# A two-layer block (attention, then a selective scan) on one core: the order of the layer norm, the score maxima, the first scan chunk and the gates is changed

## Chip, cores and metric

The kernel runs on one core of a Trainium2 chip. The metric is the device time in microseconds (us) of one execution, median over runs. The engines are PE (TensorE), DVE (VectorE), ACT (ScalarE), POOL (GpSimd) and SP (SyncE, which issues most DMAs); each takes its instructions strictly in its program's order.

## What is computed

There are 4 sequences of 256 tokens, model width 512. Layer 0 is an attention with 32 heads of latent key width 4, beside a feed-forward block of width 1792. Layer 1 is a selective scan (inner width 1024, 16 states, convolution of 4 taps), beside a top-2 mixture of low-rank experts on a dense product. The reference, cut:

```python
xn = layernorm(x)
x = x + attn(xn) + ffn(xn)
xn = layernorm(x)
x = x + scan_block(xn) + experts(xn)

# attn: scores = einsum(q, C_kv) / 2; softmax; @ V; @ Wo
# ffn:  (silu(xn @ Wg.T) * (xn @ Wu.T)) @ Wd.T
# scan_block:
xi, z = split(xn @ in_proj)               # 2 x 1024 channels
xc = silu(conv4(xi) + conv_b)
dt_r, Bm, Cm = rmsnorm of the parts of (xc @ x_proj.T)
dt = softplus(dt_r @ dt_proj.T + dt_bias)
h = exp(dt * A) * h + dt * Bm * xc        # along the 256 tokens, 1024 x 16 states
y = (sum over states of h * Cm + D * xc) * silu(z)
out = y @ out_proj.T
```

## The kernel before, in words

Everything is in one program with an order written out by hand. No scheduler moves anything: each engine runs its instructions in the order in which the code issues them. Tiles come from pools with tags; a tile with a tag and `bufs=2` takes the older of two buffers, and its first writer waits until the last readers of that buffer are done. The PSUM pool `psmm` has three buffers for most products, `pssc` two for scores.

*Layer 0.* Tokens stand in eight blocks of 128; two sequences (four blocks) are a half. Products of the feed-forward block are cut into small pieces: `gate_up(th)` and `down(th, i)` are generators, and `go(ff, n)` issues the next n pieces on PE between other work. A piece of `down` is two matmuls (hi and lo part, L454); each block of `down` begins with four matmuls of the attention's output against `m_att` (L449) and ends with an addition into x on DVE (L459).

For the softmax a maximum over the keys is needed. `scores_max` (L337, L339) makes scores of two groups of heads on PE and reduces them on DVE into `mpl`; eight steps k with two reduces each. `put_max(b, gq)` (L349, L356) transposes `mpl` with PE (`pmT`) and adds the masked maxima into `qg` on DVE; it needs two steps' maxima. `maxima(b, pieces, second, side)` runs the eight steps for a first sequence of a half with `pieces[k]` pieces of `ff` in step k; `attention(b, ff, after, step)` runs the eight steps of one sequence's softmax with the maxima of the next sequence in between.

The layer norm of a half: `ln_stats`, `ln_root` (ACT square root), `ln_scale` (DVE reciprocal L213, then one DVE instruction for each block, L216), `ln_turn` (PE transposes L225, ACT copies into `xhi` and `xnT`, L227 and L228) and `ln_rest` (DVE, `xlo`, L234). For the second half this stands after the attention of sequence 1, among the first pieces of `down(0)`, together with `normalize(1)`: four reciprocals of softmax denominators and four products on DVE (L398, L399). Then come `latents(2)` with nine pieces and `maxima(2)`.

*Layer 1.* A sequence b is worked through in 8 chunks c of 128 channels; each chunk has four steps g of four states, so a sequence has 32 scan steps (PER) and the kernel 128. A step u: `decays(u)` (four exponentials on ACT, L930), `scan_in(u)` (`bx` on DVE, L936), `scan(u)` (the scan `h` on DVE, L951, then `hc` = h times C on POOL, L955), `states_sum(u)` (`ysum` on PE, L967). After four steps `close_chunk` multiplies with the gate on DVE (`xc`, L971). A chunk's dt and du = dt*xc must lie with each channel repeated for the four states: `send` writes them to DRAM (`dtd`, `dud`) and `spread` reads them back in four DMAs each (`dts`, `dus`, L889). For the very first chunk the code before the loop instead uses PE with a selection matrix (`pdts` L1143, `pdus` L1150) and copies on DVE (L1146, L1152).

Other work is hung on steps with `put(b, s, f, ...)` and `put_late`: what is put on step s is issued around scan s, in the order of the calls, late ones after the others. For sequence 0 these are, among others: `load_z` and `pz_mm` (weights and product of the gate z, L898) and `gate_silu` (ACT, L904, with a change of the activation table before and after it, the second at L688) for chunk pairs 0 and 1; `norm_stats`, `norm_scale` (L713, tiles `xnt`), `norm_turn` (PE `pt`, L721) and `norm_copy` (L729) for the next sequence; `step_in` (PE `pdt` L820, ACT L825 and L826), `step_exp` (ACT L834 to L837) and `step_out` (POOL) for dt of the second half of the channels; `step_x` (`du` on POOL, L875); `px_mm`, `conv_in` (ACT) and `conv_taps` (DVE L761) for the next sequence. The tiles `xnt` and `du` have the same tag, `xnt`, with two buffers.

The tail of `down(1)`, for the last blocks of layer 0, is spread between the first matmuls of layer 1, and runs until the first scans are under way. SP issues the weight loads `w_in` (three buffers) in its order with the other DMAs; POOL issues those of the gate and up weights `wgu`.

In the last scan step `scan(u, parts)` is called with four parts, so that each quarter's `hc` follows that quarter's scan.

Of the kernel before, what the change touches and what calls it, by code (L numbers as in the profile page):

```python
# [8 lines left out]
F32 = mybir.dt.float32  # L9
# [3 lines left out]
ALU = mybir.AluOpType  # L13
# [4 lines left out]
P = 128  # L18
# [23 lines left out]
def block_kernel(  # L42
# [167 lines left out]

    def ln_scale(th, i, n):
        mv, rs = tok[th][2:]
        nc.vector.reciprocal(rs[:, i : i + n], rs[:, i : i + n])  # L213
        for k in range(i, i + n):
            xn = ap1.tile([P, D], F32, tag="ln_xn", name="xn", bufs=2)
            nc.vector.tensor_scalar(  # L216
                xn, x[:, 4 * th + k, :], mv[:, k, 0:1], rs[:, k : k + 1], ALU.subtract, ALU.mult
            )
            tok[th, k] = xn

    def ln_turn(th, i):
# [257 lines left out]
    def attention(b, ff, after, step, side=()):  # L479


        side = dict(side)
        for k in range(8):
            attend(b, k, 0)
            if after:
                scores_max(b + 1, k, 1 - k // 2 % 2)
            elif k:
                attend(b, k, 1)
            if after or k == 0:
                go(ff, step - step // 2)  # L490
            if k == 0:
                put_max(b, 3)
                go(ff, 3)
            elif after and k % 2 == 0:
                put_max(b + 1, k // 2 - 1)
            if after or k == 0:
                attend(b, k, 1)
            if after:
                scores_max(b + 1, k, k // 2 % 2)
            if k:  # L500
                weigh(b, k - 1)
            elif b % 2:
                weigh(b - 1, 7)
            go(ff, step // 2 if after or k == 0 else step)
            for f, *args in side.get(k, ()):
                f(*args)
# [32 lines left out]
    def maxima(b, pieces, second, side=()):  # L539

        side = dict(side)
        for k in range(8):
            for hp in range(2):
                scores_max(b, k, hp)
            for f, *args in side.get(k, ()):
                f(*args)
            go(ff, pieces[k])
            if k and k % 2 == 0:
                put_max(b, k // 2 - 1)
            go(second, 1)  # L550
        go(second)
# [17 lines left out]
    go(ff)  # L569
    ff = (0 for i in range(4) for _ in down(0, i))  # L570
    go(ff, 4)
    next(norm)
    for i in range(4):
        ln_turn(1, i)
        go(ff, 2)
        next(norm)
        if i == 1:
            ln_scale(1, 2, 2)
        ln_rest(1, i)
        go(ff, 1)  # L580
    first, second = latents(2), latents(3)
    for i in range(9):
        go(first, 1)
        go(ff, 1)
        if i == 5:
            pre_stats(0)
    maxima(2, (4, 4, 4, 6, 4, 4, 4, 4), second, {
        2: [(pre_stats, 1)], 3: [(pre_scale,)], 5: [(pre_turn, 0)], 7: [(pre_turn, 1)],
    })
    go(ff)  # L590
# [17 lines left out]
    w_of = {("x", 0, 0): weights(inx_d, 0)}  # L608
    vec = we.tile([P, DC, V_END], F32, name="vec")
    nc.sync.dma_start(vec, vec_d)  # L610
    w_of["x", 0, 1] = weights(inx_d, 2)
    w_of["x", 0, 2] = weights(inx_d, 4)
    xpw = we.tile([P, DC, 64], F32, name="xpw")
    lnw = we.tile([64, 1], F32, name="lnw")
    dtw = we.tile([RK, DIN], F32, name="dtw")
    norm = normalize(3)
    next(norm)
    go(ff, 4)
    for _ in norm:
        go(ff, 2)  # L620
    go(ff)
    ffs.close()
    ps0.close()
# [317 lines left out]
    def scan(u, parts=1):  # L941
# [7 lines left out]
        for k in range(parts):  # L949
            n = slice(k * NG // parts, (k + 1) * NG // parts)  # L950
            nc.vector.tensor_tensor_scan(  # L951
                h[:, n].rearrange("p n t -> p (n t)"), da[:, n].rearrange("p n t -> p (n t)"),
                bx[:, n].rearrange("p n t -> p (n t)"), 0.0, ALU.mult, ALU.add,
            )
            nc.gpsimd.tensor_tensor(  # L955
                hc[:, n], h[:, n],
                crows[b][:, g, :].unsqueeze(1).to_broadcast([P, NG // parts, S]), ALU.mult,
            )
# [139 lines left out]
    for i in range(2):  # L1098
# [5 lines left out]
    nc.scalar.activation(xcs[0][:, 0:6, :], xcs[0][:, 0:6, :], AF.Silu)  # L1104
    nc.scalar.activation(xcs[0][:, 6:8, :], xcs[0][:, 6:8, :], AF.Silu)
    exp_set()

    sel = w1.tile([P, KC - 1, S], F32, tag="tap", name="sel").rearrange("p k t -> p (k t)")
    nc.vector.tensor_copy(
        sel[:, 0 : NG * P].rearrange("p (k n j) -> p k n j", k=NG, n=NG),  # L1110
        ident.rearrange("p (k j) -> p k j", k=NG).unsqueeze(2).to_broadcast([P, NG, NG, NB]),
    )
    for n in range(NG):
        w = slice(n * NB, (n + 1) * NB)
        nc.scalar.activation(
# [15 lines left out]
    u, e, lw = live["u"], live["e"], live["lw"]  # L1131
    dt = dts[0, 0]
    du = w1.tile([P, 2, S], F32, tag="xnt", name="du", bufs=2)
    for j, eng in ((0, nc.vector), (1, nc.gpsimd)):
        eng.tensor_tensor(e[:, j, :], u[:, j, :], e[:, j, :], ALU.subtract)
        eng.tensor_tensor(e[:, j, :], e[:, j, :], lw[:, j, :], ALU.add)
        eng.tensor_tensor(dt[:, j, :], dt[:, j, :], e[:, j, :], ALU.add)
        eng.tensor_tensor(du[:, j, :], dt[:, j, :], xcs[0][:, j, :], ALU.mult)
    go(ff, 5)

    pdts = psx.tile([P, NG, S], F32, tag="bx", name="pdts")
    for k in range(NG):
        mm(pdts[:, k, :], lhsT=sel[:, k * P : (k + 1) * P], rhs=dt[:, 0, :], start=True, stop=True)  # L1143
    live["dts", 0, 0] = w1.tile([P, NG, S], F32, tag="dts", name="dts", bufs=2)
    live["dus", 0, 0] = w1.tile([P, NG, S], F32, tag="dus", name="dus", bufs=2)
    nc.vector.tensor_copy(live["dts", 0, 0], pdts)  # L1146
    for i in range(2):
        pdu = psmm.tile([P, 2, S], F32, tag="mm", name="pdus")
        for k in range(2):
            mm(pdu[:, k, :], lhsT=sel[:, (2 * i + k) * P : (2 * i + k + 1) * P], rhs=du[:, 0, :],  # L1150
               start=True, stop=True)
        nc.vector.tensor_copy(live["dus", 0, 0][:, 2 * i : 2 * i + 2, :], pdu)  # L1152
    for n, t in (("dt", dt[:, 1, :]), ("du", du[:, 1, :])):
        live[n, 0, 0] = scr.tile([2, P, S], F32, tag=n, name=f"{n}d")
        nc.sync.dma_start(live[n, 0, 0][1], t)
    decays(0)
    scan_in(0)
    spread("dt", 0, 1)
# [31 lines left out]
    for b in range(B):  # L1190
# [14 lines left out]
        else:  # L1205
            put(b, 1, one_out, 2)
            put(b, 1, one_step, 3)
            put(b, 2, one_out, 3)
            put_late(b, 2, load_z, b, 0)
            put_late(b, 2, lambda: send("dt", 0, 1, dts[0, 0][:, 2:4, :]))  # L1210
            put_late(b, 2, step_x, b, 1)
            put(b, 4, load_z, b, 1)
            for k, n in enumerate(("rl", "bw", "lb", "ow")):
                put(b, 9 + 2 * k, load_late, n)
            for p, u in ((0, 3), (1, 8)):
                for i in range(2):
                    put(b, u, pz_mm, b, p, i)
            put(b, 4, gate_silu, b, 0)
            put(b, 12, gate_silu, b, 1)
            put_late(b, 1, add_last, 5)  # L1220
            put_late(b, 3, add_last, 6)
            put_late(b, 4, add_last, 7)
# [23 lines left out]
        if nxt < B:  # L1246
            o = 0 if b else 1
            put(b, 0 if b else 2, norm_stats, nxt)
            put(b, 2 if b else 4, norm_scale, nxt)
            put(b, 3 if b else 5, norm_turn, nxt, 0)  # L1250
            (put if b else put_late)(b, 4 if b else 5, norm_copy, nxt, 0)
            put(b, 4 if b else 5, norm_turn, nxt, 1)
            (put if b else put_late)(b, 5, norm_copy, nxt, 1)
            for p in range(NP):
                put(b, 2 * p if b else (5, 6, 9, 9)[p], load_x, nxt, p)
                for i in range(2):
# [182 lines left out]
```

## Time and profile before

| | |
|---|---|
| time, median of 3 runs | 862.01 us (856.58 to 865.05) |
| time of the profiled execution | 866.83 us |
| its span, first to last instruction | 865.1 us |
| PE busy | 736.6 us (85%) |
| DVE busy | 685.6 us (79%) |
| ACT busy | 526.5 us (61%) |
| POOL busy | 489.6 us (57%) |
| mean granted PE clock | 0.918 |
| scans on DVE, L951 | 288.0 us in 129 instructions |
| wait of PE for hc in front of ysum | 79.2 us in 59 waits |

The time of the profiled execution is 1.7 us over its span. Lines of a timeline give the start, the duration, the engine, the source line and operation, out<-in with the shapes, how many instructions are taken together, and in square brackets the idle time of the engine before them with what ended it. Lines of the table by stage give a stretch of the span, its length, then busy time and number of instructions of PE, PE's weight loads, DVE, ACT and POOL, then the granted PE clock (1.00 is full), the share of the DMA engines and the GB/s.

### The profile page before, as it was taken

To read this page: it belongs to the slowest core of one execution; us is meant where nothing else is said; L and a number is where in the kernel's file an instruction comes from. 1 tells how busy PE (TensorE), PEld (TensorE's weight loads), DVE (VectorE), ACT (ScalarE), POOL (GpSimd) and SP (SyncE) were. 2 spreads that over 40 slices of the span, in tenths; PEclk is the share of its full clock that TensorE was granted. 3 is DMA by queue.
4 is the path that set the end of the run, shared out by engine and by line. 5 is a ranking of instruction groups with operands and counts; after the bars stand their busy time and mean duration, and the time that the engine had idled before them with its cause. 6 is when DMAs were issued, how large, how long until landed. Compare 5 with 4: busy or idle time off the path is not lost.

```text
span 865.1 us, 10769 instructions
## 1 busy us (share of the span) xinstructions
PE 736.6 (85%) x3702; PEld 411.7 (48%) x3702; DVE 685.6 (79%) x684; ACT 526.5 (61%) x1011; POOL 489.6 (57%) x377
## 2 busy tenths in 40 slices
PE   5989998989999999897877997677988778957965
PEld 3665544666555667554433454334345434312422
DVE  4687755477734437778999999999999999999995
ACT  4315574224556377687794877794976784955451
POOL 3223331001333335569759699669699659697664
PEclk9999999989999999987879899779999878988995
DMA  7234322001233323547532556233535233326200
GB/s 219 76 83 123 95 76 61 1 1 37 74 86 86 104 42 86 137 134 227 161 98 85 147 146 147 85 98 111 167 101 156 76 97 106 101 77 181 73 25 24
DMA packets 67200, 86.68 MB, mean 100 GB/s; under 512 B 12061, under 2 KB 52009, under 8 KB 66762
## 3 DMA queue, kind: packets, MB, share of 16 engines
q1 hardware_dynamic: 57786, 67.12, 27.9%
q0 software_dynamic: 9072, 18.35, 7.6%
q8 instruction: 29, 0.48, 0.2%
q10 hardware_dynamic: 288, 0.52, 0.2%
q14 instruction: 25, 0.20, 0.1%
HBM read 66.58 MB, written 10.22 MB: 89 GB/s over the span
## 4 chain that ended last, share of the span: by engine, by line
PE 42%; DVE 34%; ACT 10%; POOL 7%; issue 5%; DMA 1%; DVEq 0%; SPq 0%; ACTq 0%; POOLq 0%
DVE h L951 20%; DVE bx L936 6%; PE pg L429 6%; PE pu L429 6%; ACT decay L930 6%; PE po L454 4%; POOL hc L955 4%; PE av L382 4%; PE px L737 3%; PE pz L898 2%; PE scT L371 2%; PE ysum L967 2%; DVE mpl L339 2%; PE po L1059 2%; PE pp L781 2%
## 5 line engine op out<-in xcount | busy, mean ns | idle before, releaser
L955 POOL TENSOR_TENSOR hc<-h,cr 128x1024 f32<-128x1024 f32 (+1 forms) x131 | 302.2, 2310 | 103.3 <-DVE h L951 85.5
L951 DVE TENSOR_TENSOR_SCAN h<-decay,bx 128x1024 f32<-128x1024 f32 (+1 forms) x129 | 288.0, 2234 | 15.6 <-PE po L454 4.0
L930 ACT ACTIVATE decay<-dts,aneg 128x255 f32<-128x255 f32 x504 | 213.5, 498 | 118.9 <-DVE h L951 108.5
L967 PE MATMUL ysum<-hc,stack 128*32 128x256 f32 x1024 | 93.8, 437 | 79.6 <-POOL hc L955 79.2
L936 DVE TENSOR_TENSOR bx<-brow,dus 128x1024 f32<-128x1024 f32 x128 | 157.6, 1231 | 3.7
L441 POOL TENSOR_TENSOR hlo<-g,hhi 128x512 fp32r<-128x512 f32 x28 | 35.9, 1281 | 119.9 <-ACT hhi L440 119.9
L967 PEld LDWEIGHTS ysum<-hc,stack 128*32 128x32 f32 x1024 | 22.0, 114 | 142.7 <-POOL hc L955 123.4
L339 DVE TENSOR_REDUCE mpl<-sc 128x4 f32<-128x1024 f32 x64 | 76.7, 1219 | 12.5 <-PE sc L337 12.3
L412 POOL DMA_DIRECT2D wgu<-in_wgu x56 | 31.2, 557 | 96.9 <-PE pg L429 94.8
L373 ACT ACTIVATE pe<-scT 128x1024 f32<-128x1024 f32 x64 | 64.0, 1023 | 23.4 <-PE sc L337 15.1
L1059 PE MATMUL po<-ow,xc 128*128 128x512 f32 x128 | 73.0, 680 | 2.2 <-DVE xc L971 2.2
L898 PE MATMUL pz<-xn1T,w_in 128*128 128x256 f32 x256 | 68.0, 413 | 0.0
L737 PE MATMUL px<-xn1T,w_in 128*128 128x256 f32 x256 | 65.8, 406 | 0.8 <-ACT xn1T L729 0.8
L737 PEld LDWEIGHTS px<-xn1T,w_in 128*128 128x128 f32 x256 | 51.6, 204 | 19.3 <-issue 9.1
L898 PEld LDWEIGHTS pz<-xn1T,w_in 128*128 128x128 f32 x256 | 49.1, 201 | 19.2 <-issue 12.2
L437 DVE SCALAR_TENSOR_TENSOR g<-g,pg 128x512 f32<-128x512 f32 x28 | 19.2, 687 | 41.6 <-ACT g L436 41.6
L454 PE MATMUL po<-wd,hhi 128*128 128x512 f32 x112 | 50.6, 452 | 0.0
L429 PE MATMUL pu<-xhi,wgu 128*128 128x512 f32 x112 | 48.2, 431 | 1.8 <-DMA wgu<-in_wgu 1.8
L429 PE MATMUL pg<-xhi,wgu 128*128 128x512 f32 x112 | 48.7, 435 | 0.0
L440 ACT CAST hhi<-g 128x512 fp32r<-128x512 f32 x28 | 17.3, 619 | 48.8 <-DVE g L439 48.8
L454 PE MATMUL po<-wd,hlo 128*128 128x512 f32 x112 | 45.4, 405 | 0.0
L429 PE MATMUL pu<-xlo,wgu 128*128 128x512 f32 x112 | 45.2, 403 | 0.0
(223 smaller groups left out, 1218.5 us busy)
## 6 DMA issues: line engine op xcount, KB each, us to landing
dts<-dtd SPq DMA_DIRECT2D x124, 128.0 KB, 2.8
dus<-dud SPq DMA_DIRECT2D x124, 128.0 KB, 3.0
wgu<-in_wgu POOLq DMA_DIRECT2D x56, 256.0 KB, 2.8
w_in<-in_inx SPq DMA_DIRECT2D x16, 512.0 KB, 4.4
w_in<-in_inz SPq DMA_DIRECT2D x16, 512.0 KB, 5.5
dtd<-dt SPq DMA_DIRECT2D x15, 256.0 KB, 2.2
dud<-du SPq DMA_DIRECT2D x15, 256.0 KB, 2.2
wd<-in_wd POOLq DMA_DIRECT2D x7, 512.0 KB, 3.5
```

Source lines behind the costliest of these rows:

```text
L339: nc.vector.tensor_reduce(mpl2[b % 2][:, qb, 2 * hp : 2 * hp + 2, 16 + 2 * gq : 18 + 2 * gq], sc.rearrange("p i (f k) -> p i f k", f=2), A ...
L373: nc.scalar.activation(pes[b, k][:, 2 * t : 2 * t + 2, :], sc, AF.Exp)
L429: mm(ps, lhsT=wgus[i][:, hc, :], rhs=xs[j][:, hc, :], start=(hc == 0 and j == 0), stop=(hc == HC - 1 and j == 1))
L454: mm(po, lhsT=hids[th][j][:, m, i * P : (i + 1) * P], rhs=wd[:, m, :], start=False, stop=(m == MC - 1 and j == 1))
L737: mm(px[:, i, :], lhsT=w[:, i, hc, :], rhs=xns[b][:, hc, :], start=(hc == 0), stop=(hc == HC - 1))
L898: mm(pz[:, i, :], lhsT=w[:, i, hc, :], rhs=xns[b][:, hc, :], start=(hc == 0), stop=(hc == HC - 1))
L930: nc.scalar.activation(da[:, k, 1:], live["dts", b, c][:, k, 1:], AF.Exp, scale=aneg[:, c, k, g : g + 1])
L936: nc.vector.tensor_tensor(bx, brow[g // 2][:, g % 2, :].unsqueeze(1).to_broadcast([P, NG, S]), live["dus", b, c], ALU.mult)
L951: nc.vector.tensor_tensor_scan(h[:, n].rearrange("p n t -> p (n t)"), da[:, n].rearrange("p n t -> p (n t)"), bx[:, n].rearrange("p n t -> ...
L955: nc.gpsimd.tensor_tensor(hc[:, n], h[:, n], crows[b][:, g, :].unsqueeze(1).to_broadcast([P, NG // parts, S]), ALU.mult,)
L967: mm(ysum[k * NB : (k + 1) * NB, :], lhsT=stack, rhs=hc[:, k, :], start=False, stop=(g == NU - 1))
L1059: mm(live["po", b, i], lhsT=xcs[b][:, c, i * P : (i + 1) * P], rhs=late_w["ow"][:, c, :], start=False, stop=(c == DC - 1))
```

## The change

1. In `attention` and `maxima` the three later `put_max` calls come at k = 3, 5 and 7 instead of 2, 4 and 6.
2. Second half of layer 0's norm: one reciprocal for all four blocks; the blocks 2 and 3 are scaled on ACT (new function `ln_scale_act`) and not on DVE. `normalize(1)` is run to its end before the transposes, with nine pieces of `down(0)` in between; each transposed block is followed by three pieces.
3. `maxima(2)` runs with 26 pieces instead of 34.
4. The calls that load the second and third `w_in` tile come between the steps of `normalize(3)`.
5. The first chunk's dt and du go through DRAM like the others; the selection matrix, its 16 matmuls and the three copies are gone.
6. For sequence 0, `norm_scale` of the next sequence comes late in step 2, ahead of `step_x`, instead of in step 4; `norm_turn` in step 4 for both blocks; the second `load_z` in step 3 instead of 4, its `pz_mm` in step 5 instead of 8, its `gate_silu` in step 7 instead of 12.
7. In `scan` the last part's `hc` is made on DVE when a step is run in four parts.

```diff
@@ -210,12 +210,27 @@
 
     def ln_scale(th, i, n):
         mv, rs = tok[th][2:]
-        nc.vector.reciprocal(rs[:, i : i + n], rs[:, i : i + n])
+        if th == 0 or i == 0:
+            m = n if th == 0 else 4
+            nc.vector.reciprocal(rs[:, i : i + m], rs[:, i : i + m])
         for k in range(i, i + n):
             xn = ap1.tile([P, D], F32, tag="ln_xn", name="xn", bufs=2)
             nc.vector.tensor_scalar(
                 xn, x[:, 4 * th + k, :], mv[:, k, 0:1], rs[:, k : k + 1], ALU.subtract, ALU.mult
             )
+            tok[th, k] = xn
+
+    def ln_scale_act(th, i, n):
+
+        mv, rs = tok[th][2:]
+        sh = ap1.tile([P, 4], F32, tag="ln_sh", name="sh")
+        nc.vector.scalar_tensor_tensor(
+            sh[:, 0:n], mv[:, i : i + n, 0], -1.0, rs[:, i : i + n], ALU.mult, ALU.mult
+        )
+        for k in range(i, i + n):
+            xn = ap1.tile([P, D], F32, tag="ln_xn", name="xn", bufs=2)
+            nc.scalar.activation(xn, x[:, 4 * th + k, :], AF.Identity, bias=sh[:, k - i : k - i + 1],
+                                 scale=rs[:, k : k + 1])
             tok[th, k] = xn
 
     def ln_turn(th, i):
@@ -491,7 +506,7 @@
             if k == 0:
                 put_max(b, 3)
                 go(ff, 3)
-            elif after and k % 2 == 0:
+            elif after and k in (3, 5, 7):
                 put_max(b + 1, k // 2 - 1)
             if after or k == 0:
                 attend(b, k, 1)
@@ -545,7 +560,7 @@
             for f, *args in side.get(k, ()):
                 f(*args)
             go(ff, pieces[k])
-            if k and k % 2 == 0:
+            if k in (3, 5, 7):
                 put_max(b, k // 2 - 1)
             go(second, 1)
         go(second)
@@ -569,22 +584,23 @@
     go(ff)
     ff = (0 for i in range(4) for _ in down(0, i))
     go(ff, 4)
-    next(norm)
+    for n in (1, 2, 2):
+        for _ in range(n):
+            next(norm)
+        go(ff, 3)
     for i in range(4):
         ln_turn(1, i)
-        go(ff, 2)
-        next(norm)
         if i == 1:
-            ln_scale(1, 2, 2)
+            ln_scale_act(1, 2, 2)
+        go(ff, 3)
         ln_rest(1, i)
-        go(ff, 1)
     first, second = latents(2), latents(3)
     for i in range(9):
         go(first, 1)
         go(ff, 1)
         if i == 5:
             pre_stats(0)
-    maxima(2, (4, 4, 4, 6, 4, 4, 4, 4), second, {
+    maxima(2, (4, 3, 3, 5, 3, 3, 3, 2), second, {
         2: [(pre_stats, 1)], 3: [(pre_scale,)], 5: [(pre_turn, 0)], 7: [(pre_turn, 1)],
     })
     go(ff)
@@ -608,16 +624,16 @@
     w_of = {("x", 0, 0): weights(inx_d, 0)}
     vec = we.tile([P, DC, V_END], F32, name="vec")
     nc.sync.dma_start(vec, vec_d)
-    w_of["x", 0, 1] = weights(inx_d, 2)
-    w_of["x", 0, 2] = weights(inx_d, 4)
     xpw = we.tile([P, DC, 64], F32, name="xpw")
     lnw = we.tile([64, 1], F32, name="lnw")
     dtw = we.tile([RK, DIN], F32, name="dtw")
     norm = normalize(3)
     next(norm)
     go(ff, 4)
-    for _ in norm:
+    for i, _ in enumerate(norm):
         go(ff, 2)
+        if i in (1, 3):
+            w_of["x", 0, i // 2 + 1] = weights(inx_d, i + 1)
     go(ff)
     ffs.close()
     ps0.close()
@@ -952,7 +968,8 @@
                 h[:, n].rearrange("p n t -> p (n t)"), da[:, n].rearrange("p n t -> p (n t)"),
                 bx[:, n].rearrange("p n t -> p (n t)"), 0.0, ALU.mult, ALU.add,
             )
-            nc.gpsimd.tensor_tensor(
+
+            (nc.vector if k == NG - 1 else nc.gpsimd).tensor_tensor(
                 hc[:, n], h[:, n],
                 crows[b][:, g, :].unsqueeze(1).to_broadcast([P, NG // parts, S]), ALU.mult,
             )
@@ -1104,12 +1121,6 @@
     nc.scalar.activation(xcs[0][:, 0:6, :], xcs[0][:, 0:6, :], AF.Silu)
     nc.scalar.activation(xcs[0][:, 6:8, :], xcs[0][:, 6:8, :], AF.Silu)
     exp_set()
-
-    sel = w1.tile([P, KC - 1, S], F32, tag="tap", name="sel").rearrange("p k t -> p (k t)")
-    nc.vector.tensor_copy(
-        sel[:, 0 : NG * P].rearrange("p (k n j) -> p k n j", k=NG, n=NG),
-        ident.rearrange("p (k j) -> p k j", k=NG).unsqueeze(2).to_broadcast([P, NG, NG, NB]),
-    )
     for n in range(NG):
         w = slice(n * NB, (n + 1) * NB)
         nc.scalar.activation(
@@ -1131,28 +1142,19 @@
     u, e, lw = live["u"], live["e"], live["lw"]
     dt = dts[0, 0]
     du = w1.tile([P, 2, S], F32, tag="xnt", name="du", bufs=2)
+    for n in ("dt", "du"):
+        live[n, 0, 0] = scr.tile([2, P, S], F32, tag=n, name=f"{n}d")
     for j, eng in ((0, nc.vector), (1, nc.gpsimd)):
         eng.tensor_tensor(e[:, j, :], u[:, j, :], e[:, j, :], ALU.subtract)
         eng.tensor_tensor(e[:, j, :], e[:, j, :], lw[:, j, :], ALU.add)
         eng.tensor_tensor(dt[:, j, :], dt[:, j, :], e[:, j, :], ALU.add)
+        nc.sync.dma_start(live["dt", 0, 0][j], dt[:, j, :])
         eng.tensor_tensor(du[:, j, :], dt[:, j, :], xcs[0][:, j, :], ALU.mult)
+        nc.sync.dma_start(live["du", 0, 0][j], du[:, j, :])
+        if j == 0:
+            spread("dt", 0, 0)
+            spread("du", 0, 0)
     go(ff, 5)
-
-    pdts = psx.tile([P, NG, S], F32, tag="bx", name="pdts")
-    for k in range(NG):
-        mm(pdts[:, k, :], lhsT=sel[:, k * P : (k + 1) * P], rhs=dt[:, 0, :], start=True, stop=True)
-    live["dts", 0, 0] = w1.tile([P, NG, S], F32, tag="dts", name="dts", bufs=2)
-    live["dus", 0, 0] = w1.tile([P, NG, S], F32, tag="dus", name="dus", bufs=2)
-    nc.vector.tensor_copy(live["dts", 0, 0], pdts)
-    for i in range(2):
-        pdu = psmm.tile([P, 2, S], F32, tag="mm", name="pdus")
-        for k in range(2):
-            mm(pdu[:, k, :], lhsT=sel[:, (2 * i + k) * P : (2 * i + k + 1) * P], rhs=du[:, 0, :],
-               start=True, stop=True)
-        nc.vector.tensor_copy(live["dus", 0, 0][:, 2 * i : 2 * i + 2, :], pdu)
-    for n, t in (("dt", dt[:, 1, :]), ("du", du[:, 1, :])):
-        live[n, 0, 0] = scr.tile([2, P, S], F32, tag=n, name=f"{n}d")
-        nc.sync.dma_start(live[n, 0, 0][1], t)
     decays(0)
     scan_in(0)
     spread("dt", 0, 1)
@@ -1207,16 +1209,17 @@
             put(b, 1, one_step, 3)
             put(b, 2, one_out, 3)
             put_late(b, 2, load_z, b, 0)
+            put_late(b, 2, norm_scale, nxt)
             put_late(b, 2, lambda: send("dt", 0, 1, dts[0, 0][:, 2:4, :]))
             put_late(b, 2, step_x, b, 1)
-            put(b, 4, load_z, b, 1)
+            put(b, 3, load_z, b, 1)
             for k, n in enumerate(("rl", "bw", "lb", "ow")):
                 put(b, 9 + 2 * k, load_late, n)
-            for p, u in ((0, 3), (1, 8)):
+            for p, u in ((0, 3), (1, 5)):
                 for i in range(2):
                     put(b, u, pz_mm, b, p, i)
             put(b, 4, gate_silu, b, 0)
-            put(b, 12, gate_silu, b, 1)
+            put(b, 7, gate_silu, b, 1)
             put_late(b, 1, add_last, 5)
             put_late(b, 3, add_last, 6)
             put_late(b, 4, add_last, 7)
@@ -1246,11 +1249,12 @@
         if nxt < B:
             o = 0 if b else 1
             put(b, 0 if b else 2, norm_stats, nxt)
-            put(b, 2 if b else 4, norm_scale, nxt)
-            put(b, 3 if b else 5, norm_turn, nxt, 0)
-            (put if b else put_late)(b, 4 if b else 5, norm_copy, nxt, 0)
-            put(b, 4 if b else 5, norm_turn, nxt, 1)
-            (put if b else put_late)(b, 5, norm_copy, nxt, 1)
+            if b:
+                put(b, 2, norm_scale, nxt)
+            put(b, 3 if b else 4, norm_turn, nxt, 0)
+            (put if b else put_late)(b, 4, norm_copy, nxt, 0)
+            put(b, 4, norm_turn, nxt, 1)
+            (put if b else put_late)(b, 5 if b else 4, norm_copy, nxt, 1)
             for p in range(NP):
                 put(b, 2 * p if b else (5, 6, 9, 9)[p], load_x, nxt, p)
                 for i in range(2):
```

## Prediction

> **What bounds the kernel now.** I read the page first, then the busy time by stage, then the timelines of the engines around each edit.
>
> ```profile
> PE 736.6 (85%) x3702; PEld 411.7 (48%) x3702; DVE 685.6 (79%) x684; ACT 526.5 (61%) x1011; POOL 489.6 (57%) x377
> PE 42%; DVE 34%; ACT 10%; POOL 7%; issue 5%; DMA 1%; DVEq 0%; SPq 0%; ACTq 0%; POOLq 0%
> ```
>
> ```profile
> 131.00:152.00 21.00, 18.26 (x83) 10.43 (x76) 11.53 (x21) 8.85 (x15) 1.97 (x3) 1.00 0.22 60
> 152.00:202.00 50.00, 46.15 (x233) 32.10 (x231) 30.91 (x44) 10.92 (x20) 0.00 (x0) 0.90 0.00 1
> 283.00:356.00 73.00, 70.06 (x298) 51.05 (x297) 40.21 (x56) 41.29 (x86) 30.02 (x44) 1.00 0.32 85
> 356.00:420.00 64.00, 51.75 (x271) 32.59 (x269) 54.48 (x44) 53.45 (x109) 50.89 (x34) 0.83 0.64 185
> 420.00:850.00 430.00, 345.17 (x1704) 168.28 (x1704) 411.85 (x327) 302.74 (x636) 332.12 (x181) 0.89 0.39 106
> ```
>
> The columns are PE, PEld, DVE, ACT, POOL, clock, DMA. Up to 356 PE sets the pace (70.06 of 73 us). From 420 on DVE does (411.85 of 430), so a delay at the start of the scan is not won back. Between lies the entry, 356 to 420, where no engine is full and waits decide. I call 355.46, where PE ends its down loop and starts pz, T0.
>
> ```profile
> 186.07 0.44 PE L349 MATMUL pmT<-cst,mpl 128*128 128x128 f32 x2 [1.80 <-DVE mpl L339]
> 336.43 1.88 PE L449 MATMUL po<-m_att,o8n 128*128 128x512 f32 x4
> 341.34 0.64 PE L967 MATMUL ysum<-hc,stack 128*32 128x256 f32 x8
> 355.46 3.62 PE L898 MATMUL pz<-xn1T,w_in 128*128 128x256 f32 x16
> 374.45 3.72 PE L898 MATMUL pz<-xn1T,w_in 128*128 128x256 f32 x16
> ```
>
> ```profile
> 355.72 2.29 DVE L951 TENSOR_TENSOR_SCAN h<-decay,bx 128x1024 f32<-128x1024 f32 x1 [3.95 <-PE po L454]
> 361.24 2.28 DVE L951 TENSOR_TENSOR_SCAN h<-decay,bx 128x1024 f32<-128x1024 f32 x1
> 380.54 0.42 DVE L971 TENSOR_TENSOR xc<-ysum,sz 128x256 f32<-128x256 f32 x1 [4.72 <-PE ysum L967]
> 385.82 2.29 DVE L951 TENSOR_TENSOR_SCAN h<-decay,bx 128x1024 f32<-128x1024 f32 x1
> ```
>
> Scan 4 cannot start before T0, scan 5 starts at T0+5.8, and scan 10 at T0+30.4. The second pz, at 374.45, stands in front of the ysum for which DVE waits 4.72.
>
> **The change, part by part** (us; minus is a gain).
>
> *Maxima a step later.* A put_max transposes maxima whose second half comes from the reduces of its step. At k=3, 5, 7 those are still the two newest reduces (1.18 each). PE waits for them 5.1 in all (the waits view), and two score buffers make PE wait for reduces anyway. In the first maxima loop the transposes now stand behind 6, 5 and 4 pieces instead of 1, 1 and 5; of one wait of 2.2 I take 0.6 (bounds −2.5 to +0.5).
>
> *Second half of the norm.* Before, PE waited 0.52, 0.94 and 0.51 for xlo and 0.78 for x between 141 and 149, because four reciprocals (0.95) with products (0.29) stood among DVE's norm work. Now they come first, covered by nine pieces. Blocks 2 and 3 go to ACT, 0.81 each by its Identity rows on such tiles, and DVE loses 2×0.5. The latents start at about 153.3 instead of 151.1, with 25 pieces done instead of 16: 9×0.46 = 4.15, less 2.2, is −1.9. The third maxima loop gets 26 pieces for 34 and took 37.7; with those 4.15 gone DVE is its bound (16 reduces 18.7, adds, copies and products 9, and the waits at its ends), some 31.4. Of the 6.3, 4.15 are the pieces counted already and 1.0 returns as m_att in the latents loop: −1.1. Together −3.0 (bounds −6 to −0.5). With maxima, **−3.6** (−8 to 0).
>
> *Weight loads 2 and 4 later.* The order of SP's instructions and their waits are the same in both programs: **0**. If the loads did start later, PE's one wait of 1.8 for wgu at 289.14 might go: −1.8.
>
> *First chunk through DRAM.* PE loses 16 matmuls: 3.5 on PE's path. DVE loses 2.5 of copies and the 0.4 selector. Instead SP issues two more stores and eight more reads. Chunk 1 made that trip already:
>
> ```profile
> 331.24 0.34 SPq L1155 DMA_DIRECT2D dtd<-dt  x1
> 332.05 0.32 SPq L1155 DMA_DIRECT2D dud<-du  x1
> 332.96 1.76 SPq L889 DMA_DIRECT2D dts<-dtd  x4
> 334.81 1.32 SPq L889 DMA_DIRECT2D dus<-dud  x3
> ```
>
> Its dts had landed at 337.09 and its dus at 339.40, 5.85 and 8.16 after the first issue. DVE's dt ends at 327.77, so dts is there at 333.7 and dus at 336.0. decays(0) on ACT then ends at 335.5, and behind it in ACT's queue stands the copy cr, which frees the psmm buffer that PE's m_att needs: PE runs dry at 332.9 and goes on at 336.15, against 336.43. So the 3.5 turn into a wait. h0 moves from 334.55 to 337.4, its hc (2.29+2.37) ends at 342.1, and PE waits there for ysum until 342.1 instead of 341.34. The end of the loop comes at T0 **+1.0** (from −3.5, if ACT's queue frees cr in time, to +2.7, if the clock falls).
>
> Here the clock matters. After the wait of 1.80 at 186.07 the granted clock fell, while after the 1.80 at 289.14 it stayed at 1.00:
>
> ```profile
> 186.60:193.40 6.80, 6.73 (x28) 5.66 (x28) 3.35 (x6) 0.59 (x1) 0.00 (x0) 0.50 0.00 0
> 287.50:291.00 3.50, 1.86 (x8) 1.42 (x8) 3.47 (x4) 1.11 (x2) 1.27 (x1) 1.00 0.07 20
> ```
>
> One stretch of 3.4 at half clock costs 1.7 where PE is the bound; that is the +2.7, and the sum would be 868.2 instead of 866.5. Of two waits of one length one did it; I take no fall and keep the bound. The Trainium skill, "TensorE: Matmul & The Clock Gate", section "What's actually happening", lets the clock fall only after an idle window of about 3.4 us, by which 3.25 of idle would leave the sum at 866.5; but the wait of 1.80 at 186.07 is far short of that window and the clock fell, so the trace does not bear the rule out.
>
> *The gates and the norm of the next half at the entry.* xnt and du share two buffers. norm_scale now comes ahead of step_x, so POOL's du (1.28) waits for PE's transposes pt, which stand behind pz (3.55) and a ysum (0.55). Counted from the loop's new end: pt done 4.7, du 6.1. Behind du on POOL stand the memsets of two decay tiles, hc3 and hc4 (2.37 each); on SP the store of du, the second load of pz weights, and chunk 2's reads. hc3 ends at 8.7, its ysum at 9.2, xc at 9.6, so scan 5 starts at 9.6 instead of 5.8: +3.8. That is not the worst. The weight load issues at 6.6. This load took 4.08 and 6.63 in the two rows of the entry; the second, at 352.43, ran beside reads like these, and I take it: 13.2. PE reaches that pz in its fifth step, idle from 9.2, ends it at 16.7, and only then makes the pdt that ACT needs. ACT's ledger follows. Before, it ran without a pause from 355.66 to the taps of conv_in, which end at 382.88 (T0+27.4). Now xnt leaves (−1.5), the second silu with two table loads comes in (1.28+0.60+1.28 = +3.2), and ACT stands still from 9.5 to 17.3 (+7.8): 36.9. DVE had covered 1.5 of ACT's lateness at 383.07, so scan 10 moves by +9.5−1.5 = **+8.0**. The bounds: +5, with the short landing; +11.5, with a half-clock pz (+3.5). The gain, the second pz out of DVE's way at 380.54 (4.72), is inside this, since DVE now waits for ACT there.
>
> Later, step 12 is free of that silu: its stall of 0.35 at 400.86 goes, **−0.35** (−2.1 if the 1.73 at 411.30 went too; 0 at worst).
>
> *Last quarter on VectorE.* POOL's last quarter ends at 856.06, DVE's scan at 854.64; a quarter takes POOL 0.69, and DVE 0.42 by its products of that size (L971), so three quarters on POOL end last, at 855.4. **−0.5** (−0.7 to 0).
>
> The sum is −3.6 +1.0 +8.0 −0.35 −0.5 = +4.5. The profiled run (866.83, its span 865.1) would become 871.3; it lies above the median of 862.01, so against the median it is **866.5**.
>
> **Rivals.**
> 1. *The clock and the load go wrong together* (slower). PE's idle from 9.2 to 13.2 drops the clock for pz, and the loop has lost a stretch too: +11.5 and +2.7, with −0.5 upstream and −0.85 at the ends: 874.9. It decides once PE is idle some 4 us in front of the second pz. For it: the clock is 0.83 over 356 to 420 already. Against: the wait at 289.14 left no mark.
> 2. *The du buffer does not hold POOL* (faster). If du goes through before the transposes, the load issues as early as before, the 4.72 at 380.54 vanishes, and the entry gives −4.7: −3.6+1.0−4.7−0.85, 853.9. Against: two buffers, three tiles in that order.
> 3. *PE's saving arrives* (faster). cr is copied in time, the loop ends 3.5 earlier, upstream gives its full 8, and the entry costs its least, 5: 854.7. Against: ACT's order, decays before cr.
> 4. *The moved loads act after all*, −1.8: 864.7. Against: SP's order is unchanged.
>
> **How the numbers follow.** Chances: forecast 0.60, first rival 0.25, second 0.05, third 0.07, fourth 0.03. Three timings of the kernel before span 8.5 us, so 1% (8.6) is what a measurement can tell from no change. The forecast's own range is 861 to 871, nearly all within 1%. Slower by over 1%: 0.22 of the first rival and 0.06 of the forecast's upper end, 0.28. Faster by over 1%: some two thirds of the second and third rival, 0.09 with the forecast's lower end. The rest, 0.63, is within. The range, 857 to 877, takes in the first rival and leaves out most of the two fast ones.
>
> **What would show it.** Right: PE idle about 3 us in front of m_att of the second block of down(1); h0 near 337 less the upstream gain; DVE at scan 5 waiting for ysum or memset; ACT idle some 8 us ahead of L841; DVE waiting some 9 us for ACT's xc ahead of scan 10. Wrong: POOL's du before PE's pz; the second pz starting without a DMA wait; the distance from the first pz to scan 10 under 34 us. The latents starting no later than 151 with as many pieces, or the third maxima loop still at 37 us, would upset the upstream gain.

## Result, and the profile after

The changed kernel takes 872.25 us (median of 4 runs, 871.29 to 874.74) against 863.53 (856.58 to 868.9): a ratio of 1.0114, 95% interval 1.0069 to 1.0158. Timed again later (the run `after_again` below) it took 872.41 against 860.75, 1.0146 (1.0113 to 1.0178). It is slower by 1.1 to 1.5%.

The head of the page hides this: every engine is busy for no longer than before, or nearly so. In the chain, DVE's share fell from 34 to 31% and DMA's rose from 1 to 4%.

```profile
PE 730.9 (84%) x3686; PEld 407.1 (47%) x3686; DVE 682.0 (78%) x679; ACT 527.9 (61%) x1013; POOL 488.8 (56%) x376
PE 42%; DVE 31%; ACT 11%; POOL 6%; issue 6%; DMA 4%; SPq 0%; DVEq 0%; ACTq 0%; POOLq 0%
```

The table by stage (columns as before) shows the place. From 356 to 420 DVE is busy for 46.10 us instead of 54.48, PE for 42.17 instead of 51.75: both wait.

```profile
131.00:152.00 21.00, 20.52 (x92) 13.59 (x91) 9.94 (x18) 8.92 (x15) 1.81 (x2) 1.00 0.14 39
152.00:202.00 50.00, 45.85 (x251) 31.05 (x249) 35.27 (x51) 13.84 (x23) 0.53 (x1) 0.97 0.02 6
283.00:356.00 73.00, 68.01 (x274) 48.50 (x275) 35.83 (x47) 44.00 (x93) 27.29 (x38) 0.95 0.27 64
356.00:420.00 64.00, 42.17 (x229) 27.06 (x228) 46.10 (x39) 45.83 (x94) 46.60 (x33) 0.87 0.68 176
420.00:850.00 430.00, 343.72 (x1715) 168.07 (x1713) 412.06 (x327) 305.62 (x640) 333.64 (x185) 0.90 0.41 111
```

The timelines show who waits for whom, one fence for each engine: PE, POOL, SP, ACT, DVE.

```profile
332.26 3.67 PE L464 MATMUL po<-m_att,o8n 128*128 128x512 f32 x4 [2.85 <-ACT cr L826]
353.10 3.62 PE L914 MATMUL pz<-xn1T,w_in 128*128 128x256 f32 x16
361.73 0.64 PE L984 MATMUL ysum<-hc,stack 128*32 128x256 f32 x8 [3.42 <-POOL hc L972]
365.83 5.73 PE L914 MATMUL pz<-xn1T,w_in 128*128 128x256 f32 x16 [3.46 <-DMA w_in<-in_inz]
```

```profile
358.04 1.26 POOL L891 TENSOR_TENSOR du<-dt,xc 128x512 f32<-128x512 f32 x1 [9.94 <-PE pt L737]
359.33 4.66 POOL L972 TENSOR_TENSOR hc<-h,cr 128x1024 f32<-128x1024 f32 x2
```

```profile
359.33 0.37 SPq L899 DMA_DIRECT2D dud<-du  x1
359.87 0.35 SPq L621 DMA_DIRECT2D w_in<-in_inz  x1
```

```profile
372.71 0.47 ACT L841 ACTIVATE u<-pdt,vec 128x256 f32<-128x256 f32 x1 [10.23 <-PE pdt L836]
```

```profile
353.35 2.29 DVE L967 TENSOR_TENSOR_SCAN h<-decay,bx 128x1024 f32<-128x1024 f32 x1 [2.37 <-PE po L469]
362.85 2.28 DVE L967 TENSOR_TENSOR_SCAN h<-decay,bx 128x1024 f32<-128x1024 f32 x1
391.39 1.01 DVE L777 SCALAR_TENSOR_TENSOR px<-pad,vec,px 128x256 f32<-128x256 f32 x2 [8.28 <-ACT xc L764]
394.17 2.29 DVE L967 TENSOR_TENSOR_SCAN h<-decay,bx 128x1024 f32<-128x1024 f32 x1
```

Read in the order of causes: POOL's du waits 9.94 for the transposes pt; with it wait the hc behind it (PE 3.42 in front of ysum) and the weight load behind du's store (PE 3.46 in front of the second pz). The granted clock is 0.50 from 363.5 to 370.0, and that pz takes 5.73 instead of 3.7. ACT has had nothing to do for 10.23 when the pdt behind it comes, and DVE waits 8.28 for ACT in front of scan 10. From the first pz to scan 10 it takes 41.07 us; before, 30.36.

### The profile page after: what moved, and what is told of

Its sections match the earlier page's. It is cut to its first block, busy times and chain, and to the rows that moved or that the text cites. A ratio compares the mean times of both kernels' runs of the same rounds, so it can differ in the third digit from the quotient of the medians.

```text
span 870.9 us, 10749 instructions
## 1 busy us (share of the span) xinstructions
PE 730.9 (84%) x3686; PEld 407.1 (47%) x3686; DVE 682.0 (78%) x679; ACT 527.9 (61%) x1013; POOL 488.8 (56%) x376
## 4 chain that ended last, share of the span: by engine, by line
PE 42%; DVE 31%; ACT 11%; POOL 6%; issue 6%; DMA 4%; SPq 0%; DVEq 0%; ACTq 0%; POOLq 0%
DVE h L967 18%; DVE bx L952 6%; PE pg L444 6%; ACT decay L946 6%; PE pu L444 6%; PE po L469 5%; POOL hc L972 4%; PE av L397 4%; PE pz L914 3%; PE scT L386 2%; PE px L753 2%; PE ysum L984 2%; DVE mpl L354 2%; PE po L1076 2%; PE po L464 2%
## 5 line engine op out<-in xcount | busy, mean ns | idle before, releaser
L984 PE MATMUL ysum<-hc,stack 128*32 128x256 f32 x1024 | 91.7, 429 | 92.1 <-POOL hc L972 91.7
```

The lines of the kernel that those rows point to most:

```text
L984: mm(ysum[k * NB : (k + 1) * NB, :], lhsT=stack, rhs=hc[:, k, :], start=False, stop=(g == NU - 1))
```

## Experiments

Executions of one program differ by more than 10 us here (856.81 to 868.31 in 31 runs of the kernel before), so the experiments are read in two ways: by the median over the runs, and by distances between marks inside a profile. The marks are the end of DVE's dt of the first chunk (end of layer 0 and of what leads to the scan), the first pz (end of PE's loop of down pieces), scan 10 and scan 17. Each number is a difference of two start times (for dt an end) in a timeline. The ratio is to the kernel before as it was timed together with that row; its medians were 860.95 for gates_undone, order_swapped, chunk_by_pe and front_only, 861.99 for du_own_tag, silu_at_12, cr_first and joined, and 860.75 for after_again and entry_only. So medians of different rows are compared by their ratios.

| kernel | end of dt | dt to first pz | first pz to scan 10 | scan 10 to 17 | median us | ratio to before, interval |
|---|---|---|---|---|---|---|
| before | 327.77 | 27.69 | 30.36 | 32.05 | | |
| before_again_1 | 324.09 | 27.72 | 28.82 | 30.23 | 856.96 (one run) | |
| before_again_2 | 328.34 | 27.67 | 28.81 | 30.21 | 863.58 (one run) | |
| after | 324.02 | 29.08 | 41.07 | 29.75 | 872.25 | 1.0114, 1.0069 to 1.0158 |
| after_again | 328.38 | 30.58 | 41.44 | 29.75 | 872.41 | 1.0146, 1.0113 to 1.0178 |
| gates_undone | 325.18 | 29.08 | 28.80 | 30.22 | 863.30 | 1.0010, 0.9981 to 1.0039 |
| order_swapped | 322.29 | 28.80 | 32.04 | 29.75 | 865.29 | 1.0027, 0.9994 to 1.0059 |
| du_own_tag | 323.95 | 29.19 | 32.04 | 29.76 | 862.22 | 1.0025, 0.9993 to 1.0056 |
| silu_at_12 | 328.65 | 30.47 | 28.70 | 30.22 | 864.29 | 1.0025, 0.9995 to 1.0055 |
| chunk_by_pe | 325.34 | 27.66 | 40.68 | 29.76 | 870.94 | 1.0094, 1.0055 to 1.0133 |
| cr_first | 328.78 | 30.23 | 28.80 | 30.22 | 865.88 | 1.0056, 1.0027 to 1.0086 |
| front_only | 325.31 | 27.69 | 30.61 | 30.54 | 862.73 | 0.9998, 0.9966 to 1.0030 |
| joined | 330.71 | 27.71 | 27.40 | 31.68 | 861.26 | 0.9987, 0.9958 to 1.0015 |
| entry_only | 325.21 | 27.71 | 27.39 | 30.21 | 858.99 | 0.9984, 0.9950 to 1.0018 |

**The entry undone: gates_undone.**

```diff
-            put_late(b, 2, norm_scale, nxt)
-            put(b, 3, load_z, b, 1)
+            put(b, 4, load_z, b, 1)
-            for p, u in ((0, 3), (1, 5)):
+            for p, u in ((0, 3), (1, 8)):
-            put(b, 7, gate_silu, b, 1)
+            put(b, 12, gate_silu, b, 1)
 (and norm_scale, norm_turn, norm_copy for sequence 0 as before)
```

> The changed kernel with its sixth part undone: norm_scale of the next sequence, the second load_z, its pz and its gate stand again where the kernel before has them. Theory (the entry of the scan is lost to du waiting on POOL for the transposes, because norm_scale stands ahead of step_x): from the loop's end (first pz) to scan 10 it takes 30.4 us as before instead of 41.1, the small gains of steps 11 to 17 (2.3) go too, so the time falls from 872.3 by 8.4 to about 864. Rival (the first chunk's way through DRAM is what costs): no more than 2 us of change, 870 to 874.

28.80 from the first pz to scan 10, and 863.30: the loss goes with this one part, to within the interval. Steps 10 to 17 lose 0.5 by it (30.22 for 29.75) and not the 2.3 expected. That 2.3 and the 30.4 were read from the first profile of the kernel before alone; its other two have 30.2 and 28.8.

**The order of two lines: order_swapped.**

```diff
-            put_late(b, 2, norm_scale, nxt)
             put_late(b, 2, lambda: send("dt", 0, 1, dts[0, 0][:, 2:4, :]))
             put_late(b, 2, step_x, b, 1)
+            put_late(b, 2, norm_scale, nxt)
```

> The changed kernel with one line moved: norm_scale stands behind step_x in late step 2, not ahead of it; the loads and gates stay where the change put them. Theory (it is the order of the two users of the shared buffers): POOL's du runs at about 348 and waits for no transpose, the second pz starts without a DMA wait, ACT stands still no 10 us ahead of its L841, scan 10 comes 30 to 31 us after the first pz, and the later gains stay: 861 to 863. Rival (the second gates moved to step 7 load ACT, whatever the order): scan 10 still 35 us or more after the first pz, 866 or more.

```profile
356.80 3.72 PE L914 MATMUL pz<-xn1T,w_in 128*128 128x256 f32 x16
```

```profile
361.68 0.47 ACT L841 ACTIVATE u<-pdt,vec 128x256 f32<-128x256 f32 x1 [1.20 <-PE pdt L836]
```

```profile
380.35 1.01 DVE L777 SCALAR_TENSOR_TENSOR px<-pad,vec,px 128x256 f32<-128x256 f32 x2 [5.91 <-ACT xc L764]
```

POOL's du runs at 346.44 without a wait, the second pz (PE) starts without one and at full clock, ACT stood still 1.20 instead of 10.23, and the distance falls from 41.1 to 32.04. It is more than the 30 to 31 expected, for DVE still waits 5.91 for ACT's xc: the theory has most of it and the rival, whose 35 us are not reached, may have the rest. The median of 865.29 lies over the 861 to 863 expected.

**The buffer, with the order left: du_own_tag.**

```diff
-        du = w1.tile([P, 2, S], F32, tag="xnt", name="du", bufs=2)
+        du = w1.tile([P, 2, S], F32, tag="du", name="du", bufs=1)
```

> The changed kernel; only the du tiles of step_x get a buffer of their own instead of sharing the tag xnt. norm_scale stays ahead of step_x. Theory (it is the shared buffer that holds POOL, not the place of norm_scale): POOL's du runs at about 346 to 348 without waiting for PE's pt, the second pz starts without a DMA wait, scan 10 comes 31 to 33 us after the first pz instead of 41.1, time 862 to 867 like the kernel with the order swapped. Rival (the early norm itself fills ACT or SP's queue at the wrong place): still 869 or more.

```profile
348.15 1.29 POOL L891 TENSOR_TENSOR du<-dt,xc 128x512 f32<-128x512 f32 x1
```

32.04, to the hundredth the distance of the kernel with the order swapped, and POOL's du runs without a wait, with norm_scale still ahead of it. So it is the shared buffer, not the early norm: 9.0 us.

**The silu of the second gate: silu_at_12** (order_swapped, and in addition):

```diff
-            put(b, 7, gate_silu, b, 1)
+            put(b, 12, gate_silu, b, 1)
```

> The kernel with the order swapped, and the second gate's silu back in step 12 (its pz stays in step 5). Theory (ACT sets scan 10: its silu with two table loads costs 3.2 there): scan 10 comes 28.9 to 29.5 us after the first pz instead of 32.0, a wait of 0.3 to 2 for ACT returns at the conv taps of steps 12 to 14, and the time is 1 to 3 us under that of the kernel with the order swapped (865.3). Rival (pz held in its PSUM buffer from step 5 to 12 leaves PE two buffers and stalls it): scan 10 no earlier than 32 after the first pz.

```profile
385.04 1.01 DVE L777 SCALAR_TENSOR_TENSOR px<-pad,vec,px 128x256 f32<-128x256 f32 x2 [2.58 <-ACT xc L764]
```

32.04 falls to 28.70, by 3.3; the silu with its two table loads has 1.28+0.60+1.28 = 3.2. DVE's wait for ACT falls by as much. Steps 10 to 17 give 0.5 back. The rival, 32 or more, is out. The expected 1 to 3 us do not show in the times: the ratios are 1.0025 and 1.0027, with intervals that overlap, for the spread of the runs is larger.

**The first chunk by PE again: chunk_by_pe.** The changed kernel with the selection matrix, its 16 matmuls and three copies as in the kernel before.

> The changed kernel with its fifth part undone: the first chunk's dt and du are spread by PE and a selection matrix again. Theory (the DRAM way costs the loop 1.35 us and little else): the loop ends at 351.5 to 352 in the profile instead of 353.1, no wait of PE for cr, and the time is 870 to 871.5. Rival (the DRAM way is the main loss): 866 or less.

PE's m_att runs without a wait (1.88 for four at 333.97), and dt to first pz takes 27.66 instead of 29.08, so the way through DRAM costs 1.4 in that profile; in the seven profiles that have it 1.1 to 2.9 more than 27.7. The loop's end was expected at 351.5 to 352 and came at 353.0, since dt itself ended 1.3 later. The time fits, 870.94, and the rival's 866 is not reached.

**The copy cr ahead of the exponentials: cr_first** (on gates_undone).

```diff
-    decays(0)
     scan_in(0)
     ...
     c_rows(0, 1)
+    decays(0)
     decays(1)
```

> The changed kernel with the sixth part undone, and the rows of B and C (with ACT's copy cr) issued before decays(0) instead of behind it. Theory (PE's wait of 2.9 for cr is only the first of two: behind it PE waits for hc of scan 0, which the DRAM way sets): the wait in front of m_att goes, PE waits 3 us or more in front of the first ysum instead, the first pz comes no more than 1 us earlier against the first scan than with the order unchanged, and the time stays within 1.5 us of 863. Rival (the wait for cr is the whole price of the DRAM way): the loop ends 3 to 4.6 earlier and the time is 858.5 to 860.

```profile
334.00 1.88 PE L464 MATMUL po<-m_att,o8n 128*128 128x512 f32 x4
338.95 0.69 PE L858 MATMUL pdt<-nrm,dtw 32*128 32x256 f32 x2 [1.22 <-ACT dt L863]
343.49 1.08 PE L984 MATMUL ysum<-hc,stack 128*32 128x256 f32 x8 [3.22 <-POOL hc L972]
```

The wait of 2.9 for cr is gone from PE's timeline; 1.22 and 3.22 stand behind it instead, and dt to first pz does not shrink (30.23, against 29.08 in gates_undone). What was late next was scan 0's hc. The time did not stay within 1.5 of 863 (865.88); its dt ended 3.6 later than in gates_undone, in layer-0 code that is the same.

**Layer 0 alone: front_only.** The kernel before with the first four parts of the change.

> The kernel before with the first four parts of the change alone (maxima, norm of the second half, pieces, place of the two weight loads). Theory (layer 0 gains 5.7 us, of which 2.0 is given back where PE waits for wgu at about 284 and the clock falls): first matmul of the following softmax at 196.3 instead of 202.0, first scan 3.7 to 5.7 earlier, and the time 3.7 to 5.7 under the kernel before in the same call. Rival (the gain of layer 0 is absorbed by the scan's entry): within 1.5 us of the kernel before.

The rival's number: 862.73 against 860.95, ratio 0.9998, interval 0.9966 to 1.0030, so a gain of 2.9 us is the most that these runs allow. The first matmul of the softmax came at 199.24, not at 196.3. In this profile scan 0 does come 2.5 earlier (332.09), yet the last scan starts at 852.94, 0.7 after that of the kernel before.

**The kernel before, again: before_again_1 and before_again_2.** Nothing is edited.

> The kernel before once more, for a second profile of it. Theory (its first profile was one draw among clock phases; 16.9 us of layer 0 ran at half clock there, and in the nine profiles of kernels with the new layer 0, whose code is one and the same, 7 to 24): the first score matmul after 185 us comes at another time than 202.0, between 197 and 203, and the sum of its half-clock time up to 203 us differs from 16.9 by 3 or more. Rival (202.0 belongs to the program): 201.5 to 202.5 again.

> The kernel before a third time, for the same reason: theory, between 197 and 203 and not the same as in the other two profiles; rival, 201.5 to 202.5.

The first line of the softmax behind the third maxima loop (PE's timeline) of the two runs, then the stage 152 to 203 of the kernel before, of before_again_1 and of joined; the third number from the right is the granted clock:

```profile
198.29 0.50 PE L371 MATMUL scT<-qg,km 32*128 32x512 f32 x2
```

```profile
202.18 0.50 PE L371 MATMUL scT<-qg,km 32*128 32x512 f32 x2
```

```profile
152.00:203.00 51.00, 47.15 (x241) 32.89 (x240) 31.78 (x46) 11.61 (x21) 0.00 (x0) 0.90 0.00 1
```

```profile
152.00:203.00 51.00, 47.15 (x259) 32.77 (x258) 34.75 (x50) 13.33 (x23) 0.53 (x1) 0.97 0.01 4
```

```profile
152.00:203.00 51.00, 47.19 (x225) 31.28 (x224) 31.74 (x46) 10.79 (x20) 0.00 (x0) 0.83 0.00 0
```

198.29 and 202.18: the theory holds for the first (7.3 us at half clock up to 203, not 16.9), the rival for the second (16.9 again). The same program reaches this point up to 3.9 apart, at a clock of 0.97 or 0.90; kernels with the new layer 0 reach it between 196.29 (after) and 202.69 (joined, clock 0.83). One profile of each cannot measure a change of a few us here.

**The best of it: joined and entry_only.** joined: layer-0 parts, first chunk by PE, norm_scale early but behind step_x, second load_z in step 3, its pz in step 8 and its silu in step 12, last quarter on DVE. entry_only is joined without the layer-0 parts.

> What the runs so far speak for, put together: the layer-0 parts, the first chunk by PE, norm_scale early but behind step_x, the second pz in step 8 and its silu in step 12, the last quarter on DVE. Theory A (the gains of layer 0 and of the entry last to the end): scan 10 28 to 29 after the first pz, the mean over the runs 2 to 4 us under the kernel before of this call. Theory B (what layer 0 gains is lost again to a lower granted clock further on, as in the kernel with the front alone): within 1.5 us of the kernel before, at a mean clock 0.003 or more below its.

> The joined kernel without the layer-0 parts: the kernel before with norm_scale of the next sequence early behind step_x, its turns in step 4, the second load_z in step 3, and the last quarter on DVE. Theory A (layer 0's edits are worth nothing over many runs, the entry and the tail give what the joined kernel has): mean 860 to 861.5, 1 to 2 under the kernel before. Theory B (the layer-0 edits are worth 2 or more): 862.5 or more, no better than the kernel before.

Both enter the scan 1.4 faster than the kernel before at its better (27.40 and 27.39 against 28.81). Their times, 861.26 and 858.99, are 0.1 to 0.2% under the kernel before, with intervals that hold 1. Of joined's theories the first fell short (its mean, 860.92, is 1.35 under the 862.27 of the kernel before, and 0.8 under it without that kernel's three longest runs) and the numbers of the second hold (mean clock 0.9243 against 0.9280); that the clock is the cause, they do not show. entry_only's mean, 859.93, is a little under the range of theory A: with a ratio of 0.9984 for it and 0.9987 for joined, the layer-0 parts are worth nothing that these runs can tell.

**The changed kernel again: after_again.**

> The changed kernel once more, timed on the same chip as the kernel before and the others of this call. Theory: 870.5 to 873.5, a ratio of 1.010 to 1.013 to the kernel before, first pz in another place than 353.1 by 1 us or more, but 40 to 42 us between it and scan 10 again. Rival (the long entry was a matter of the clock phase in that one profile): 37 or less.

The first pz came 5.9 later than in the first profile, and still 41.44 lie between it and scan 10. The long entry is the program's, not the draw's.

## Why the prediction was right, and where not

The direction, and a time inside the range, were right; the chance was not well placed. I gave 0.63 to a change within 1% and 0.28 to slower by more, and slower by 1.1 to 1.5% it was. The measured time, 872.3, lies nearer to the first rival's 874.9 than to the forecast's 866.5, and it lies in the range because the range was drawn to take in that rival. Two terms of the sum were off, and both made the forecast too fast: the entry's loss was taken 4.3 too small, layer 0's gain 3.6 too large.

*The entry, +8.0.* The mechanism stood step by step: du behind the transposes, hc and the weight load behind du, ACT idle, DVE waiting for ACT. The size is 41.1−28.8 = 12.3. order_swapped, du_own_tag and silu_at_12 find 9.0 for the buffer and 3.3 for the silu. What is left is two effects that cancel: the early norm, with the load in step 3, brings 1.4 (entry_only, 27.39 for 28.8), and silu_at_12, whose second pz stays in step 5, is 1.3 slower than joined, which has it in step 8. joined also spreads the first chunk by PE, but that alone moves this distance by 0.4 to 0.8 in the changed kernel and by nothing in gates_undone, so the 1.3 is put down to the pz, without a run for it alone.

The ledger of ACT gives nearly the same: −1.5 +3.2 +10.2 = 11.9. What was mis-sized: ACT's idle was 10.2, not 7.8, mostly because the clock fell for part of the second pz. The prediction had 3.55 for it; it took 5.32 in chunk_by_pe, 5.73 in after and 6.49 in after_again, and the entries are 40.68, 41.07 and 41.44. And the 1.5 taken off for DVE's cover was no cover. The first profile's entry of 30.36 held 1.5 that the other two (28.82, 28.81) lack: between 364 and 375 its granted clock was 0.53, where before_again_1 had 1.00 and before_again_2 0.84, and its second pz came 19.0 after the first instead of 15.5 and 15.6. DVE's wait of 4.72 at 380.54, which the prediction books as a gain of this part, is 1.17 and 1.31 in the other two. The first rival had the fall of the clock at the second pz right, on a wait of 3.46 where it asks for some 4, and I had called it the less likely; its price for the pz, 3.5, was 2.2.

*Layer 0, −3.6.* In the first profile after, dt ends 3.75 earlier than before, close to the forecast, and that was luck. Over all profiles it ends at 326.4 in the mean of four with the old layer 0 and at 326.3 in the mean of ten with the new, and front_only is not faster. The term that was mis-sized is "took 37.7": of the time of that loop, the third of the maxima, 3.4 was due to a clock of 0.50 in that execution, and the sum took it for the program's. before_again_1 passed the loop at full clock in 34.6; without the 3.4 the sum's −3.6 reads −0.2.

The waits named went only in part. Those for xlo (2.0) and for x in front of m_att (0.8) are no longer in the waits of PE. That for the maxima in front of the transposes moved to the scores, 5.6 in all before and 4.9 after, near the 0.6 that the prediction took. The waits of PE (us in total, times, longest), two rows of before and two of after:

```profile
PE pmT L349 <- DVE mpl L339: 5.1, 4, 2.2
PE sc L337 <- DVE mpl L339: 0.5, 1, 0.5
PE sc L352 <- DVE mpl L354: 4.6, 8, 1.0
PE pmT L364 <- DVE mpl L354: 0.3, 1, 0.3
```

So the edits do save time of PE, and in these ten profiles a lower clock takes it back. The ten profiles had 17.0 us at half clock ahead of the end of dt, in the mean, and the four old ones 12.7 (each stage's length times twice its missing clock, summed). With half of each profile's own sum taken off, dt ends at 319.3 to 320.5 in the four and at 316.4 to 318.8 in the ten, 2.3 earlier in the mean: an estimate. Whether the new order lowers the clock, or the draws fell so, ten profiles don't settle; that a gain of 3.6 does not reach the end of the kernel, front_only's twelve runs show.

*The first chunk, +1.0.* Measured +1.1 to +2.9, 1.9 in the mean of the seven profiles; the upper end is a little over its bound of 2.7. The wait in front of m_att came as worked out (2.85 to 3.24 for 3.25), and the saving of 3.5 went into it. The least, +1.1, is order_swapped, where the clock stayed at 1.00 behind that wait. cr_first shows that a second wait stood behind it.

*The weight loads, 0.* PE's wait for wgu stayed (2.1 instead of 1.8 in the profile after; after_again and before_again_1 have none); no run tried a real delay of the loads.

*Steps 12 and on, −0.35.* 30.2 from scan 10 to 17 becomes 29.75: −0.5.

*The last quarter, −0.5.* From the last scan's end to the last xc 2.57 became 2.16 in the first two profiles: −0.4. But with POOL's quarter it is 2.13 in before_again_1 and 2.27 in front_only, and in the mean of four 2.39, against 2.12 in the mean of ten with DVE's: −0.3. DVE's quarter took more than the 0.42 assumed:

```profile
860.62 0.91 DVE L972 TENSOR_TENSOR hc<-h,cr 128x256 f32<-128x256 f32 x1
```

With these in place of the prediction's terms the sum reads 0 +1.9 +12.3 −0.5 −0.3 = +13.4; measured, 872.41−860.75 = +11.7 and 872.25−863.53 = +8.7. The profiles alone close better: the stretches of the two of the changed kernel, less those of the three of the kernel before, in the mean, are −0.5 (to the end of dt), +2.1, +11.9, −1.1 and −0.5 (from scan 17 to the end of the span), +11.9 in all. Nearly all of it is the entry.

## What to carry to other kernels

When two producers share a tag, the order in which they are issued decides which waits; before moving one ahead of the other, list what is queued behind the one that will wait, on its engine and on the DMA queue that stores its result. Here 9 us hung on the order of two lines, and a separate buffer of 2 KB per partition undoes it as well as the order does. And before a wait is counted as a gain, look whether the clock was full in that stage: a stage seen once at half clock promises gains that no other execution has, while a distance between two marks that repeats to a tenth in several profiles can be trusted against a time that wanders by more than 10 us.

## What was not expected of the hardware

The granted clock in one and the same program differs from execution to execution: 0.918 to 0.938 in 17 runs of the kernel before, and its times with it, 867.07 at 0.918 and 856.52 at 0.938.

Waits of PE under 3.3 us stand in front of several of its falls, but a wait does not decide alone. Behind the 1.80 at 186.07 the clock fell to 0.50; before_again_1 waited as long at the same instruction and kept 1.00. Behind the wait in front of m_att it fell in the profile after (2.85; the four matmuls took 3.67) and in after_again (3.24; 3.78), and not in order_swapped, which waited 2.94 (1.98, at a clock of 1.00); cr_first, without the wait, took 1.88. The rows of before_again_1 and of order_swapped:

```profile
185.40 0.44 PE L349 MATMUL pmT<-cst,mpl 128*128 128x128 f32 x2 [1.79 <-DVE mpl L339]
```

```profile
330.62 1.98 PE L464 MATMUL po<-m_att,o8n 128*128 128x512 f32 x4 [2.94 <-ACT cr L826]
```

In front of the second pz of the profile after, the clock fell within the first us of the wait of 3.46 (0.56 over 363 to 364), behind the one of 3.42. The Trainium skill, "TensorE: Matmul & The Clock Gate", section "What's actually happening", asks for at least one idle window of about 3.4; the 1.80 and the 2.85 here were shorter, and the clock fell.

DVE's quarter, 0.91, began at 860.62 while POOL's third quarter ran until 861.26, so 0.27 of it lay behind POOL's end. The Trainium skill, "SBUF — State Buffer", section "Who interferes with whom", says that a DVE instruction with two SBUF inputs contends with a GpSimd instruction that reads SBUF, and calls it an exclusive lock; the row fits that. No run here took POOL's part away, so it is not shown to be the cause.
